# A replanned order of work, and layer 0's statistics partly by batch-norm instructions, in a two-layer residual block kernel

## Chip, core and metric

The kernel runs on one core of one Trainium2 chip. The metric is the time of one execution on the device, in microseconds (us). Five engines work side by side, each through its own queue of instructions in order: TensorE (PE; PEld is its weight load), VectorE (DVE), ScalarE (ACT), GpSimd (POOL) and SyncE (SP), which here issues nearly all transfers.

## What is computed

x has 128 batches of 128 rows by 512 columns in fp32; adj is 128 x 128. Layer 0 mixes rows, takes the row maximum and normalizes; layer 1 is masked attention with 8 heads over the 128 rows, a projection, an inner layer norm, and an outer one.

```
# layer 0: W1 = W2 = adj, so C - A is the bias and the same in every column
A   = adj @ x[b];  C = adj @ x[b] + b0
out = max over n of relu(A[n] + (C - A)[m])      # = relu(rowmax(A) + b0)
x   = layernorm(x + out)                          # out is one number per row
# layer 1
qkv = x @ w_qkv;  attn = softmax(mask(adj, q k^T / 8));  o = (attn v) @ w_proj + b_proj
x   = layernorm(x + o + layernorm(o) * gamma + beta)
```

## The kernel before

**Tiles and groups.** Batches go in 32 groups of four. For each batch: `conv` (L186) multiplies adj^T by x into one PSUM bank `pa`; `conv_max` (L190, DVE) takes the row maximum into `rm`; `relu_0` (L196, POOL) adds the bias. `add_0` (L202, ACT) adds rm to x in place and sums the row; `stats_0` (L484, ACT) makes the sum of squared deviations; `rstd_0` and `shift_0` (L213 to L225, L490, L491, POOL) make scale and shift for a pair of batches; `norm_0` (L232, ACT) applies them. `x_halves` (L244, ACT) writes x as two planes of 16-bit halves into the one buffer `xplanes`, SP stores them to DRAM (`rowsx`), and `crossbar_x` (L250, SP) brings them back transposed into an `xt` buffer. `split_x` (L261, L263 on DVE; `split_high`, L268 on POOL or L270 on ACT; `split_d`, L275 on POOL or DVE) makes the three forms of x (h, l, d) whose products stand for one fp32 product. In group 0 PE transposes x instead (`transpose_x`, L239), and `product_v` (L289) makes two of the values in plain fp32.

**Products.** `dense` (L309, L310, L317) makes for each group eight products of 512 columns for q and k (j = 4 to 11) and four for the values v (j = 0 to 3). Each has two PSUM banks, from the pool `ps_1` (four banks: names pm, pd) or `ps_2` (two buffers of two banks: name pp). `dense_main` (L344, ACT) and `dense_rest` (L348, DVE) empty them. `project` (o products) uses the same form, emptied by `projected_main` and `projected_rest` (DVE).

**Attention.** `scores` (L359, into `psc`), `masked` (L371, DVE: scale and add the mask), `row_max` (L379, DVE), `exps` (L386, ACT, eight of them), `weights` (L394, L395, DVE), `halves` (L401, ACT: planes of the weights, stored by SP as `rows`), `crossbar_T` (L410, SP: transposed back as `eT`), `attend` (L432, into `pav`), `heads` (a split of pav). In the last group PE transposes the weights (`transpose_e`, L419; `weights_T`, L423, ACT).

**End of layer 1.** `residual` reloads x (`xb`), `residual_x` (L455, L456, POOL) normalizes it again with the kept scale and shift and adds beta, `residual_o` (L473) adds o on POOL, in the last group on DVE. `stats` (squares on ACT, small operations on POOL), `norm_1` (L503, L478, DVE) and `norm_2` (L511, ACT, then the store by SP) finish.

**The order.** Nothing is left to a scheduler: every step is put into a list with a place in us by `at(place, f, ...)`, the list is sorted, and the steps are issued in that order on all engines' queues. PE's steps are laid end to end with the lengths in `LENGTH` (56.1 us a group in the plan), after `dense_order`, `pair_order` and `tail_order`. All other steps are placed relative to a PE step by the numbers in the table `O`, one per position in the group, and clamped so that nothing stands ahead of what it needs. `O["two"]` chooses engines and PSUM pools. A group's period in the plan runs from dense product (g, 4) to (g + 1, 4). In it PE does dense 4, 5, two convolutions, dense 6, 8, 7, 11, 10, 9, then attention, scores, dense 0 to 3 and four projections of two groups before, with the other two convolutions just ahead of the last.

**Buffers that couple queues.** `xt` has four buffers that x and its transposed form take in turn, so that the load of the next group's first x is placed right behind the group's fourth `crossbar_x`; `xplanes` and `planes` have one, `eT` two, `o` three (shared with the weights' raw tiles at the start).

Of the kernel before, what the change touches and what calls it, by code (L numbers as in the profile page):

```python
# [18 lines left out]
EPS = 1e-5  # L19
# [7 lines left out]
def tile_adj_resnorm_d2(  # L27
# [198 lines left out]

    def norm_0(b, vector=False):
        rstd, nm = norms.pop((b, 0))
        if vector:
            nc.vector.tensor_scalar(xs[b], xs[b], rstd, nm, op0=ALU.mult, op1=ALU.add)  # L230
            return
        nc.scalar.activation(xs[b], xs[b], AF.Identity, bias=nm, scale=rstd)  # L232
# [117 lines left out]
    def scores(b):  # L350
# [4 lines left out]
        pscs[b] = psc = ps_2.tile([P, 2, HP, P], FP, tag="ps2", name=f"psc_{b}")  # L355
        for hp in range(HP):
            for s in range(2):
# [3 lines left out]
                    start=True, stop=True,  # L361
                )

    def masked(b):
        if b < B - 1:
            e = work.tile([P, H, P], FP, tag="e", bufs=3, name=f"e_{b}")
        else:

            e = work.tile([P, 2, H * P], U16, tag="planes", bufs=1, name=f"e_{b}")
            e = e.rearrange("p s m -> p (s m)").bitcast(FP).rearrange("p (h m) -> p h m", h=H)  # L370
        nc.vector.scalar_tensor_tensor(  # L371
# [3 lines left out]
        es[b] = e  # L375

    def row_max(b):
        nmax = small.tile([P, H], FP, tag="nmax", name=f"nmax_{b}")
        nc.vector.tensor_reduce(nmax, es[b], AX.X, ALU.max, negate=True)  # L379
        es[b] = es[b], nmax  # L380

    def exps(b):
        e, nmax = es[b]
        sums = small.tile([P, H], FP, tag="sums", name=f"sums_{b}")
        for j in range(H):
            nc.scalar.activation(  # L386
                e[:, j, :], e[:, j, :], AF.Exp, bias=nmax[:, j : j + 1],
                accum_out=sums[:, j : j + 1],
# [82 lines left out]
    def residual_o(b):  # L471
        engine = nc.gpsimd if b < B - G else nc.vector
# [35 lines left out]
    def norm_2(b):  # L508
# [9 lines left out]
    O = {'add_0': [-28.01, -2.67, 12.08, -40.74],  # L518
 'conv_max': [4.55, 4.72, 6.29, 4.66],
 'dense_order': [('dense', 4), ('dense', 5), ('conv', 3), ('conv', 2), ('dense', 6), ('dense', 8),  # L520
                 ('dense', 7), ('dense', 11), ('dense', 10), ('dense', 9)],
 'final': {'norm_1': [5.56, 10.5, 14.34, 13.61],
           'norm_2': [12.82, 25.73, 75.6, 26.29],
           'residual': [-18.87, -9.5, -3.43, -8.74],
           'residual_o': [5.36, 6.15, 8.98, 4.31],
           'residual_x': [-41.8, -51.69, -15.49, -25.59],
           'stats_1': [5.17, 9.89, 7.71, 8.6],
           'stats_2': [12.28, 13.13, 19.78, 20.53]},
 'last': {'norm_1': [9.58, 9.14, 7.67, 8.6],
          'norm_2': [13.12, 22.67, 13.86, 10.82],  # L530
          'residual': [-2.72, -10.61, 6.62, -30.79],
          'residual_o': [3.24, 7.11, 7.11, 5.39],
          'residual_x': [-30.28, -1.34, -16.65, -32.32],
          'stats_1': [5.84, 4.73, 7.43, 4.32],
          'stats_2': [9.71, 14.36, 12.44, 9.12]},
 'load': [0.06, -0.01, -14.55, -3.61],
# [300 lines left out]
```

## Time and profile before

| | us |
|---|---|
| median of 3 runs | 1988.98 (1987.63 to 1991.59) |
| profiled execution, its own time | 1980.06 |
| its span | 1978.3 |
| dense product (3, 4) starts | 205.80 |
| dense product (31, 4) starts | 1869.74 |

| stretch, us | PE busy | DVE | ACT | POOL | granted clock |
|---|---|---|---|---|---|
| 0 to 205.8 | 174.65 | 157.83 | 156.07 | 97.92 | 0.98 |
| 205.8 to 1869.7 | 1605.23 | 1384.11 | 1410.46 | 1157.93 | 1.00 |
| 1869.7 to 1978.3 | 80.28 | 75.98 | 58.64 | 72.64 | 0.89 |

How its lines are read: in a wait, the engine and what it was to work on stand left of the arrow, what ended its idle time right of it; then us in total, how often, the longest. In a line of the timeline, start and length in us, engine (q for its queue), source line, operation, output and inputs, and in brackets the idle time before it with what ended it. In a line of groups, the count, then busy us in total and mean ns of one, then the idle time before them. An engine's output that the next engine takes up costs nothing as long as PE finds it in time.

### The profile page before, as it was taken

The page shows a single profiled execution, that of the slowest core. Times are in us where ns is not written, and L with a number is a line of the kernel's source. Part 1 is how long each engine was busy: PE and PEld are TensorE (multiplying, and loading weights), DVE is VectorE, ACT ScalarE, POOL GpSimd, SP SyncE. Part 2 cuts the span into 40 slices and gives each one's busy share as a digit, 9 for nine tenths or more (in the row PEclk, how much of TensorE's full clock was granted, in tenths as well). Part 3 has the DMA queues.
Part 4 walks back from the last instruction along what each step waited for, and adds up shares of the span by engine and source line. Part 5 has one row for each costly group of instructions (what it writes and reads, how often), then busy time and mean ns, then how long its engine had stood idle before and what let it go on. Part 6 is the DMA issues. An engine that isn't in the chain of part 4 may idle for free.

```text
span 1978.3 us, 33244 instructions
## 1 busy us (share of the span) xinstructions
PE 1860.2 (94%) x10537; PEld 1435.6 (73%) x10537; DVE 1617.9 (82%) x2485; ACT 1625.2 (82%) x4158; POOL 1328.5 (67%) x1970
## 2 busy tenths in 40 slices
PE   7799999999999999999999999999999999999995
PEld 4577777777777777777777777777777777777773
DVE  6788888878888888888878888877788878888885
ACT  5788888888888788888888888888888888878763
POOL 4166767766677766777766767766767766767767
PEclk9999999999999999999999999999999999999997
DMA  4465556665665665566675566665565675665541
GB/s 129 101 171 145 159 162 160 155 172 152 148 162 161 159 181 150 150 162 159 161 181 149 154 165 164 160 172 144 155 158 159 165 179 145 159 154 159 137 118 48
DMA packets 486144, 302.94 MB, mean 153 GB/s; under 512 B 399440, under 2 KB 403664, under 8 KB 485969
## 3 DMA queue, kind: packets, MB, share of 16 engines
q1 hardware_dynamic: 485104, 299.70, 58.5%
q8 instruction: 84, 1.38, 0.3%
q10 hardware_dynamic: 864, 1.12, 0.2%
q14 instruction: 92, 0.75, 0.1%
HBM read 72.16 MB, written 131.07 MB: 103 GB/s over the span
## 4 chain that ended last, share of the span: by engine, by line
PE 61%; ACT 14%; DVE 10%; DMA 8%; issue 5%; POOL 2%; SPq 0%; DVEq 0%; ACTq 0%; POOLq 0%
PE pa L186 5%; ACT e L386 4%; DMA xt<-in_x_dram 3%; DMA rowsx<-xplanes 2%; ACT xplanes L244 2%; ACT planes L401 2%; PE psc L359 2%; PE pav L432 2%; DMA eT<-rows 2%; ACT xt L232 2%; ACT square L484 1%; DVE x_l L263 1%; DVE xh L261 1%; DVE v L348 1%; DVE e L371 1%
## 5 line engine op out<-in xcount | busy, mean ns | idle before, releaser
L386 ACT ACTIVATE e<-e,nmax 128x128 f32<-128x128 f32 x1024 | 396.2, 391 | 74.1 <-DVE nmax L379 74.1
L490 POOL TENSOR_SCALAR sum<-sum 128x1 f32<-128x1 f32 (+1 forms) x322 | 102.1, 317 | 203.6 <-ACT square L484 188.4
L401 ACT COPY planes<-e 128x2048 uint16<-128x2048 uint16 x124 | 234.1, 1888 | 1.8 <-issue 1.8
L491 POOL TENSOR_TENSOR sum<-sum,mhalf 128x1 f32<-128x1 f32 (+1 forms) x322 | 212.8, 661 | 26.8
L484 ACT ACTIVATE square<-o,sum 128x512 bf16<-128x512 f32 x256 | 183.5, 717 | 24.1 <-DVE o L478 22.4
L386 ACT ACTIVATION_READ_ACCUMULATOR e<-e,nmax 128x1 f32 x1024 | 194.7, 190 | 0.0
L456 POOL TENSOR_TENSOR xb<-xb,beta_sb 128x512 f32<-128x512 f32 x128 | 176.9, 1382 | 10.7
L395 DVE TENSOR_TENSOR e<-e,sums 128x1024 f32<-128x1024 f32 x128 | 173.7, 1357 | 4.4
L432 PE MATMUL pav<-eT,v 128*64 128x128 f32 x2048 | 142.3, 282 | 32.8 <-DMA eT<-rows 18.1
L496 POOL TENSOR_SCALAR sum<-sum 128x1 f32<-128x1 f32 x256 | 100.5, 392 | 101.7 <-DVE o L478 99.1
L473 POOL TENSOR_TENSOR xb<-xb,o 128x512 f32<-128x512 f32 x124 | 161.9, 1306 | 4.8
L244 ACT COPY xplanes<-xt 128x1024 uint16<-128x1024 uint16 x124 | 129.3, 1043 | 31.6 <-DMA rowsx<-xplanes 29.6
L432 PEld LDWEIGHTS pav<-eT,v 128*64 128x64 f32 x2048 | 112.1, 138 | 59.4 <-DVE x_l L263 21.9
L379 DVE TENSOR_REDUCE nmax<-e 128x8 f32<-128x1024 f32 x128 | 154.9, 1211 | 0.0
L371 DVE SCALAR_TENSOR_TENSOR e<-psc,mask 128x1024 f32<-128x1024 f32 x128 | 152.9, 1214 | 0.7 <-PE psc L359 0.7
L186 PE MATMUL pa<-xt,adjT 128*128 128x512 f32 x256 | 123.9, 607 | 25.9 <-DMA xt<-in_x_dram 16.5
L455 POOL TENSOR_SCALAR xb<-xb,sum 128x512 f32<-128x512 f32 x128 | 127.2, 994 | 25.3 <-DMA xb<-in_x_dram 24.6
L359 PE MATMUL psc<-qkT 64*128 64x128 f32 x2048 | 142.0, 284 | 1.9 <-DVE e L371 1.9
L359 PEld LDWEIGHTS psc<-qkT 64*128 64x128 f32 x2048 | 123.4, 189 | 25.4 <-issue 23.0
L213 POOL TENSOR_SCALAR sum<-sum 128x2 f32<-128x2 f32 (+1 forms) x66 | 31.2, 472 | 161.9 <-ACT xt L202 161.6
L202 ACT ACTIVATE xt<-xt,rm 128x512 f32<-128x512 f32 x128 | 91.9, 718 | 43.8 <-POOL rm L196 43.8
L511 ACT ACTIVATE o<-o,sum 128x512 f32<-128x512 f32 x128 | 100.8, 814 | 23.9 <-POOL sum L499 23.8
(4653 smaller groups left out, 5770.0 us busy)
## 6 DMA issues: line engine op xcount, KB each, us to landing
rows<-planes SPq DMA_DIRECT2D x124, 512.0 KB, 3.3
xt<-in_x_dram SPq DMA_DIRECT2D x128, 256.0 KB, 3.5
xb<-in_x_dram SPq DMA_DIRECT2D x128, 256.0 KB, 2.9
out_dram<-o SPq DMA_DIRECT2D x128, 256.0 KB, 2.4
rowsx<-xplanes SPq DMA_DIRECT2D x124, 256.0 KB, 2.5
wraw<-in_L_gnn_w_qkv_dram SPq DMA_DIRECT2D x8, 256.0 KB, 3.2
xT<-rowsx SPq DMA_TRANSPOSE x124, 3.5
eT<-rows SPq DMA_TRANSPOSE x124, 4.8
```

The source lines that it names most:

```text
L186: nc.tensor.matmul(pa[b], adjT, xs[b], start=True, stop=True)
L244: nc.scalar.copy(planes, xs.pop(b).bitcast(U16).rearrange("p (m s) -> p s m", s=2))
L359: nc.tensor.matmul(psc[:, s, hp, :], qkT[hs, hp, i, :], qkT[hs, KC + hp, i, :], start=True, stop=True,)
L371: nc.vector.scalar_tensor_tensor(e, pscs.pop(b).rearrange("p s a m -> p (s a) m"), scale, mask_b, op0=ALU.mult, op1=ALU.add,)
L386: nc.scalar.activation(e[:, j, :], e[:, j, :], AF.Exp, bias=nmax[:, j : j + 1], accum_out=sums[:, j : j + 1],)
L395: nc.vector.tensor_tensor(e, e, sums[:, :, None].to_broadcast([P, H, P]), op=ALU.mult)
L401: nc.scalar.copy(planes, e.rearrange("p h m -> p (h m)").bitcast(U16).rearrange("p (m s) -> p s m", s=2),)
L432: nc.tensor.matmul(pavs[b][s * HD : (s + 1) * HD, hp, :], v[:, h * HD : (h + 1) * HD], eT[:, s * HP + hp, :], start=True, stop=True,)
L456: nc.gpsimd.tensor_tensor(xbs[b], xbs[b], beta_sb, op=ALU.add)
L473: engine.tensor_tensor(xbs[b], xbs[b], os[b], op=ALU.add)
L484: nc.scalar.activation(square, x, AF.Square, bias=s[:, 0:1], scale=-float(D), accum_out=s[:, 1:2],)
L491: nc.gpsimd.tensor_tensor(s, s, mhalf[:, :n], op=ALU.pow)
```

## The change

Four things, of which the first is by far the longest in effect on the order:

1. Nearly every number of `O` is new, so that the steps of all engines but PE change places. PE's order stays, apart from some exchanges in the tail. In `two`, dense product 0 of a group takes its banks from `ps_2`, the first projection takes two of `ps_1`; `split_d` of the second x goes from DVE to POOL, `split_high` of the first o from POOL to ACT; at the start two engines are swapped for a copy and a norm.
2. `stats_x`, `rstd_x`, `shift_x` are new: mean and variance of x by `bn_stats` and `bn_aggr` on DVE, without first adding rm (one number per row doesn't change what the normalization gives). The first pair of every group and all of group 0 use them; the second pairs keep `add_0` and `stats_0`.
3. `scores` can put the mask into PSUM by two products of the identity with the mask, ahead of the scores; `exps` then reads PSUM and scales. The last batch alone uses it.
4. In the last group `residual_o` of the first batch goes to POOL. Loads of x are placed after all four splits of the group are known, and the statistics after the loads.

```diff
+    def stats_x(b):
+        st = small.tile([P, 6], FP, tag="bnst", bufs=2, name=f"bnst_{b}")
+        nc.vector.bn_stats(st, xs[b])
+        nc.vector.bn_aggr(mv0s[g][:, i, 0:2], st)
+
+    def rstd_x(b, n):
+        var = mv0s[g][:, i : i + n, 1]
+        nc.gpsimd.tensor_scalar(var, var, EPS, None, op0=ALU.add)
+        nc.gpsimd.tensor_tensor(var, var, mhalf[:, :n], op=ALU.pow)
+
+    def shift_x(b, n):
+        mean, rstd, both, shift = (mv0s[g][:, i : i + n, k] for k in range(4))
+        r = rms[g][:, i : i + n]
+        nc.gpsimd.tensor_tensor(both, mean, r, op=ALU.add)
+        nc.gpsimd.tensor_tensor(both, r, both, op=ALU.subtract)
+        nc.gpsimd.tensor_tensor(shift, both, rstd, op=ALU.mult)
+        for k in range(n):
+            norms[b + k, 0] = c0s[b + k] = rstd[:, k : k + 1], shift[:, k : k + 1]
...
+        if with_mask:
+            for s in range(2):
+                nc.tensor.matmul(
+                    psc[:, s], ident, mask[:, None, :].to_broadcast([P, HP, P]), start=True, stop=False,
+                )
...
-    O = {'add_0': [-28.01, -2.67, 12.08, -40.74],
+    O = {'add_0': [-38.7, -4.55, -0.42, -31.04],
...
- 'load': [0.06, -0.01, -14.55, -3.61],
+ 'load': [-20.41, 3.65, -32.28, -8.94],
...
- 'softmax': {'cross': [-12.79, -9.61, -18.95, -6.28],
-             'exps': [10.86, 9.05, 42.17, 22.92],
-             'halves': [1.11, 11.24, 0.39, 2.34],
-             'masked': [0.34, 3.01, 1.47, 17.35],
-             'row_max': [16.52, 12.06, 18.4, 20.81],
-             'weights': [10.99, 14.73, 21.85, 34.94]},
+ 'softmax': {'cross': [-11.04, -10.0, -15.2, -5.92],
+             'exps': [13.59, 24.89, 35.29, 23.69],
+             'halves': [8.19, 11.44, 0.41, 1.44],
+             'masked': [2.1, 1.22, 6.73, 16.85],
+             'row_max': [28.59, 28.53, 20.89, 20.26],
+             'weights': [9.81, 15.04, 21.31, 31.4]},
...
- 'two': {'copy': [0, 1],
-         'd': [1, 0, 1, 0, 0, 1, 0, 1],
-         'dense': [0, 0, 0, 0, 1, 0, 1, 0, 0, 0, 0, 0],
+ 'two': {'bn': [1, 0],
+         'copy': [1, 0],
+         'd': [1, 1, 1, 0, 0, 1, 0, 1],
+         'dense': [1, 0, 0, 0, 1, 0, 1, 0, 0, 0, 0, 0],
...
-         'h': [1, 0, 0, 0, 1, 1, 0, 0],
-         'norm': [1, 0, 0, 0],
-         'po': [1, 0, 1, 0]},
- 'x_cross': [-8.02, -8.17, -10.06, 4.43],
+         'h': [1, 0, 0, 0, 0, 1, 0, 0],
+         'norm': [0, 1, 0, 0],
+         'po': [0, 0, 1, 0],
+         'tail_mask': [0, 0, 0, 1],
+         'tail_vector': [0, 1, 1, 1]},
+ 'x_cross': [-8.02, -4.16, -10.12, 2.24],
...
- 'x_halves': [-7.87, -8.53, -8.31, -7.49],
+ 'x_halves': [-8.29, -11.6, -7.53, -6.86],
...
+                    if two_of("bn", 0, i // 2):
+                        done = 0.0
+                        for k in pair:
+                            q = max(min(early[k][1], limit - 1.5), loads.get(k, pe["conv", k]) + 0.1)
+                            at(q, stats_x, k)
+                            done = max(done, q)
+                        at(done + 0.1, rstd_x, pair[0], 2)
+                        done = max(done + 0.2, r + 0.1, limit - 0.1 + min(O["rstd_0"][i], 0.0))
+                        at(done, shift_x, pair[0], 2)
...
+                            if k + G < B:
+                                loads[k + G] = max(splits[k] + max(O["load"][k % G], 0.02), crossed[b // G] + 0.02)
+                                at(loads[k + G], load_x, k + G)
...
-    for b, u in splits.items():
-        if b + G < B:
-            at(max(u + O["load"][b % G], u + 0.02, crossed[b // G] + 0.02), load_x, b + G)
```

## The prediction

> **What bounds the kernel now.** I read the page's summary and slices first, then what TensorE waits for in the steady part, then one group of four batches in order of time.
>
> ```profile
> PE 1860.2 (94%) x10537; PEld 1435.6 (73%) x10537; DVE 1617.9 (82%) x2485; ACT 1625.2 (82%) x4158; POOL 1328.5 (67%) x1970
> ...
> PE   7799999999999999999999999999999999999995
> ```
>
> TensorE (PE) is the bound, and it has holes at both ends. Groups start where dense product (g, 4) starts: (3, 4) at 205.80 and (31, 4) at 1869.74 us, so 28 groups last 59.43 us each. Busy time by stretch gives PE idle 31.2 us of the first 205.8, 58.7 us of the 1663.9 between, and 28.3 us of the last 108.6. PE's own waits from 200 to 1800 us:
>
> ```profile
> PE pav L432 <- DMA eT<-rows: 15.8, 17, 2.5
> PE pa L186 <- DMA xt<-in_x_dram: 15.8, 15, 1.8
> PE pav L432 <- DVE x_l L263: 6.7, 10, 0.8
> PE pa L186 <- DVE xh L261: 5.5, 6, 1.0
> PE pa L186 <- DVE x_l L263: 3.1, 2, 1.7
> PE pm_('o', 17)_3542 L309 <- ACT v L344: 1.0, 1, 1.0
> ```
>
> With the other nine rows like the last (v, 6.1 us in all) and three of 0.2 these are 54.6 us in 26.9 groups, 2.03 a group. Three places: attention times values (pav), the convolution (pa), the second projection. A group without them would take 57.4 us. The work of PE is the same after the change, apart from the tail, so only waits can go.
>
> Why are the transfers late? Group 10 starts at 622.52; times after "+" count from there. ScalarE (ACT), SP's queue and PE:
>
> ```profile
> 646.39 1.89 ACT L401 COPY planes<-e 128x2048 uint16<-128x2048 uint16 x1
> ...
> 653.76 1.05 ACT L244 COPY xplanes<-xt 128x1024 uint16<-128x1024 uint16 x1 [1.56 <-DMA rowsx<-xplanes]
> ...
> 659.70 1.03 ACT L244 COPY xplanes<-xt 128x1024 uint16<-128x1024 uint16 x1
> ...
> 668.25 1.05 ACT L244 COPY xplanes<-xt 128x1024 uint16<-128x1024 uint16 x1
> ```
>
> ```profile
> 660.76 0.34 SPq L246 DMA_DIRECT2D rowsx<-xplanes  x1
> 661.20 1.91 SPq L410 DMA_TRANSPOSE eT<-rows  x1
> ...
> 669.43 0.52 SPq L246 DMA_DIRECT2D rowsx<-xplanes  x1
> 673.55 1.23 SPq L250 DMA_TRANSPOSE xT<-rowsx  x1
> 674.83 1.04 SPq L91 DMA_DIRECT2D xt<-in_x_dram  x2
> ```
>
> ```profile
> 666.47 1.09 PE L432 MATMUL pav<-eT,v 128*64 128x128 f32 x16 [1.38 <-DMA eT<-rows]
> ...
> 678.31 1.96 PE L186 MATMUL pa<-xt,adjT 128*128 128x512 f32 x4 [1.05 <-DMA xt<-in_x_dram]
> ```
>
> SP's queue is in order. The last eT transpose is queued behind the store of the third xplanes, which ACT starts at +37.2; the next group's load of x is queued behind the store and transpose of the fourth, which ACT starts at +45.7. Both are ACT's lateness, passed through SP: its plan places are +32.8 and +41.9.
>
> **The change, part by part.**
>
> *Statistics.* Half of the batches (the first pair of each group, and all of group 0) lose two ACT passes:
>
> ```profile
> L202 ACT ACTIVATE xt<-xt,rm 128x512 f32<-128x512 f32 x128 | 91.9, 718 | 43.8 <-POOL rm L196 43.8
> ...
> L484 ACT ACTIVATE square<-xt,sum 128x512 bf16<-128x512 f32 x128 | 92.2, 721 | 1.0
> ...
> L190 DVE TENSOR_REDUCE rm<-pa 128x1 f32<-128x512 f32 x128 | 84.5, 680 | 3.1 <-PE pa L186 3.1
> ...
> L394 DVE RECIPROCAL sums<-sums 128x8 f32<-128x8 f32 x128 | 24.7, 193 | 0.3 <-ACT e L386 0.3
> ```
>
> Each pass is 0.72 plus 0.19 for the accumulator's read, so ACT loses 4 x 0.91 = 3.6 us a group, and 0.63 gets added for one "high" split moved to it from POOL (row of L270): -3.0. VectorE (DVE) gains two statistics instructions and two aggregations, which no trace here has run. Nearest rows: the 512-wide reduction (0.68) and the 8-wide reciprocal (0.19): 2 x 0.87 = 1.74 us; two passes over the data would make 3.1, and below 2 x 0.5 (the 0.46 of the leanest 512-wide row, L261, and no aggregation) it won't go. I take 1.74. One x_d subtraction of 1.16 (mean) leaves DVE, so DVE is +0.6 on some 50 us. POOL gets that x_d (1.30), loses the high split (1.98) and about 0.4 of small operations: -1.1. All this is behind PE; it counts only through the queues below.
>
> A rule bears on this: the Trainium skill, "SBUF — State Buffer", § Who interferes with whom, has a VectorE instruction with two SBUF inputs contend with a GpSimd one that reads SBUF, and the loser blocked for the whole instruction, while one with a single SBUF input outside the two-port modes does not contend. The trace fits the first half: x_d on DVE takes 0.68 at least and up to 1.72. The rule speaks against moving a further x_d to POOL: if it blocks one DVE instruction for all its length, DVE's +0.6 becomes +1.9; by the rows' means, which hold such blocking already, it stays +0.6. I take the rows; the statistics instruction, with one input, adds no blocking by the rule, which no row here shows.
>
> *ACT's order.* In the new order the halves of the previous softmax (1.8 us) go before +23.4 and not after it. From the same point, the last qkT eviction (645.90, +23.4), the new ACT queue up to the third xplanes is: eviction 0.5, norm 0.8, xplanes 1.0 (to +25.7), an add 0.8, a final norm 0.7, a square 0.8, the high split 0.6, norm 0.8 (to +29.3), xplanes 1.0 (its predecessor's store, issued +25.8, takes 2.5 to 3.6, so the 1.56 wait is gone), eight exps 3.1 from +30.3 (their row maximum was at +30.1), norm 0.7: the third xplanes starts at +34.1, 3.1 us earlier. Transpose issued at +35.7, landing after the 5.1 us that it took here (661.20 to 666.34): +40.8. PE, without its earlier waits, wants it at 665.09 - 0.52 = +42.05. The shortage of 1.4 becomes a slack of 1.2.
>
> On: eviction 0.5, exps from +36.6 (row maximum as before) to +39.7, eviction 0.5, square 0.8, norm 0.8: fourth xplanes at +41.8, 3.9 earlier. Softmax halves (1.8) now follow it, and their 512 KB store slips into SP ahead of the transpose; SP is then waiting for the xplanes store anyway. Store issued at +42.9 and landed at +47.0 (4.1 as before, 669.43 to 673.49), transpose 1.3, load at +48.3, landed +51.7 (3.35 as before); PE wants it at +52.84 (678.31 less the waits 1.05, 1.38, 0.52). Slack 1.1.
>
> Here a second rule gives another sum: "DMA: Bandwidth & Descriptors", § Anatomy of one DMA (stated for the GpSimd path), has a fixed 2.0 us plus bytes by 436 GB/s, 2.6 us for 256 KB. The page's list of issues has 3.5 for the load (nine in ten land by 3.8), 4.8 for eT (by 5.3). By the rule the load would have 1.9 us of slack and the later halves would be free; by the row 1.1, which a store in its way can use up now and then. I take the row.
>
> *New waits.* The second projection now waits for evictions of the first on DVE (planned 3 us before it) rather than for ACT's v: its 7.1 us go. The third projection now needs the buffer that the third mask-add frees, and that has moved behind other DVE work. From the row maximum's end (659.13, +36.6): weights 2.2, two evictions 0.6 each, split of x 1.1, v 0.6, projection 0.6, weights 1.5, heads 1.3, norm 1.5, split 0.9, split of x 1.1, mask-add 1.1: done at +49.7, wanted at +50.0. Level, so 0 to 1 us; I take 0.3.
>
> Sum per group: 2.03 off, 0.3 on, and 0.4 for landings beyond the slack: -1.3 us, for 28 groups -36. Bounds: -0.3 and -1.9.
>
> *Start.* The four layer-0 statistics leave ACT, but two of them stand on DVE ahead of adjT's copy, waiting for x 1 (landed 5.62): the first convolution moves from 4.83 to about 7.7. Against it, norms no longer wait for squares. Batch 0's norm follows its weight split on ACT, about 13.4; value product at about 17, as now (17.02). First dense product as now: 0. Then PE waits of 3.2, 1.4 and 3.0 for qkT evictions behind xplanes copies on ACT, which come earlier now: I take 5 of 7.6 off, bounds +3 and -12 with the other waits of groups 1 and 2.
>
> *Tail.* PE's largest wait (4.87 at 1936.80, for eT's copy behind a square that waited for DVE) loses that square; the 2.33 for POOL's high split moves to ACT. The mask of the last batch by PE adds two matrix products of the convolution's size, 2 x 0.86 = 1.7, and takes 1.2 off DVE. A final norm now stands ahead of that copy and can take some back. Of 7.2 I keep 6.7 - 1.7 = 5; bounds +4 and -14.
>
> Sum: 36 + 5 + 5 = 46. The profiled execution took 1980.06 us (span 1978.3), so 1934; the three runs' median is 8.9 above it, 1988.98 - 46 = **1943 us**.
>
> **Rivals.**
> - *Only half of it* (DVE becomes the limit). For: DVE is 83% busy in the middle stretch, would be 87%, and the mask-add has no slack. Against: it is idle about 10 us a group. At -0.5 a group, 14, and half of the ends, 5: 1970.
> - *It doesn't do what it says.* The load is still issued right behind the last transpose, with the same planned 2.1 us before its convolution; if ACT's order isn't what makes it late, the waits stay. For: the plan places; against: the 3 to 4 us of ACT above. Ends alone: 1984.
> - *Slower: the mask-add.* Ahead of it in DVE's queue stands the split of the second x, whose transpose the plan now issues 4 us later. If that stops DVE, everything behind (v, heads, evictions) is late, and PE at projection 3. Against: SP should issue it at about +38, for a use at +47.5. From 1.7 us of lateness per group (the 1.3 gained, 0.3 and the ends' 10/28) the change loses; at 3 us more, +47 net of the rest: 2026.
>
> **How the numbers follow.** Forecast 0.70, with its own range 1925 to 1957; half 0.17 (1957 to 1980); no effect 0.06 (1980 to 1993); slower 0.06; better than 1925 0.01. The range of 8 in 10, 1922 to 1973, leaves out the last two and part of the third. 0.2% (4 us) is about what a measurement tells from no change: faster (under 1985) 0.90, same 0.04, slower 0.06.
>
> **What would show it.** Groups of about 58.1 us; PE's waits for eT and xt under 10 us together from 200 to 1800; the third and fourth xplanes copies some 3 us earlier after dense (g, 4); statistics instructions near 0.7 us; the third projection waiting for DVE's e a few tenths; no 4.9 us wait for eT's copy in the tail. Wrong if projection 3 waits over 1.5 us a group, if the load still lands after its convolution's turn with ACT on time, or if DVE's queue is late throughout.

## The result, and the profile after

The changed kernel takes 1970.53 us (median of 4 runs, 1967.99 to 1971.78), the kernel before beside it 1990.28 (4 runs, 1987.63 to 1991.8): a ratio of 0.9901, 95% interval 0.9883 to 0.9918, 19.8 us less. 46 were forecast. On another chip the same pair gave 1968.49 and 1982.49, ratio 0.993 (0.9906 to 0.9954). Single runs of the kernel before lie between 1973 and 1995 us in one session, those of the changed kernel within 7 us; a pair of profiled executions therefore says less than the ratio. The profiled executions differ by 8.3 us of span only (1978.3 and 1970.0), since that of the kernel before was some 9 us faster than its median.

Summary and slices of the changed kernel's page, which answer to those of before:

```profile
PE 1868.6 (95%) x10541; PEld 1434.7 (73%) x10541; DVE 1647.6 (84%) x2585; ACT 1548.3 (79%) x3926; POOL 1244.1 (63%) x1935
...
PE   6799999999999999999999999999999999999995
```

ACT is busy for 76.9 us less and GpSimd for 84.4 less, DVE for 29.7 more. Dense product (3, 4) starts at 207.13 us (before 205.80), (31, 4) at 1864.83 (1869.74): 28 groups of 59.20 us each in place of 59.43. The start lost 1.3 us, the groups gained 6.2 and the tail 3.4.

TensorE's waits from 200 to 1800 us, changed kernel (us in total, times, longest):

```profile
PE pav L471 <- DMA eT<-rows: 9.7, 14, 1.7
PE pd_('o', 71)_11834 L344 <- POOL od L302: 1.6, 1, 1.6
PE pav L471 <- ACT xplanes L271: 1.4, 1, 1.4
PE pav L471 <- ACT xt L259: 1.3, 4, 0.4
PE pd_('o', 27)_4992 L344 <- POOL od L302: 1.0, 1, 1.0
PE pd_('o', 95)_15566 L344 <- POOL od L302: 1.0, 1, 1.0
```

The waits of the convolution for x and of the second projection for v are gone, that of the attention product is smaller. A new one stands in every group: the difference product of the fourth projection waits 1.0 us for od of GpSimd, 25.8 us in groups 3 to 28.

Group 10 after the change starts at 620.85 us. ScalarE:

```profile
646.33 0.81 ACT L259 ACTIVATE xt<-xt,sum 128x512 f32<-128x512 f32 x1 [1.43 <-POOL sum L250]
...
656.50 1.05 ACT L271 COPY xplanes<-xt 128x1024 uint16<-128x1024 uint16 x1
...
663.05 1.05 ACT L271 COPY xplanes<-xt 128x1024 uint16<-128x1024 uint16 x1
```

SP's queue, and TensorE in the same stretch:

```profile
658.01 2.05 SPq L449 DMA_TRANSPOSE eT<-rows  x1
...
667.92 2.07 SPq L91 DMA_DIRECT2D xt<-in_x_dram  x2
```

```profile
663.03 1.09 PE L471 MATMUL pav<-eT,v 128*64 128x128 f32 x16 [0.29 <-ACT xt L259]
673.72 1.88 PE L186 MATMUL pa<-xt,adjT 128*128 128x512 f32 x4
```

The third xplanes copy starts at +35.65 (before +37.2, forecast +34.1), the fourth at +42.2 (+45.7, forecast +41.8). The load of x is issued at +47.1 and has landed at +52.3, ahead of its convolution at +52.87, which has no wait. The last eT lands at +42.05, just too late. ScalarE's first norm of the group stands 1.43 us for GpSimd's shift, one of 27 such waits (39.4 us from 200 to 1800), and all that follows on ScalarE is late by it. GpSimd's queue shows why: the shift's last operation is the second line, behind one that waited 5.51 us for ScalarE.

```profile
643.35 0.19 POOL L529 TENSOR_SCALAR sum<-sum 128x1 f32<-128x1 f32 x1 [5.51 <-ACT square L523]
...
646.11 0.20 POOL L250 TENSOR_TENSOR sum<-sum 128x2 f32<-128x2 f32 x1
```

The end of the same group, GpSimd and then TensorE:

```profile
675.72 1.30 POOL L302 TENSOR_TENSOR x_d<-x_h,x_l 128x512 fp32r<-128x512 f32 x1 [0.70 <-ACT x_h L297]
676.98 1.44 POOL L302 TENSOR_TENSOR od<-oh,ol 128x512 fp32r<-128x512 f32 x1
```

```profile
678.48 1.19 PE L344 MATMUL pd_('o', 39)_6858<-p_d,od 128*128 128x512 f32 x4 [1.02 <-POOL od L302]
```

The difference of the third x now stands ahead of od in GpSimd's queue. In the plan od is at 4.84 us before the next group and x_d at 4.87; before the change od was first (-5.04 and -4.94).

### The profile page after: what moved, and what is told of

The parts are those of the page before. It is cut to its first block, busy times and chain, and to the rows that moved or that the text cites. A ratio compares the mean times of both kernels' runs of the same rounds, so it can differ in the third digit from the quotient of the medians.

```text
span 1970.0 us, 32988 instructions
## 1 busy us (share of the span) xinstructions
PE 1868.6 (95%) x10541; PEld 1434.7 (73%) x10541; DVE 1647.6 (84%) x2585; ACT 1548.3 (79%) x3926; POOL 1244.1 (63%) x1935
## 4 chain that ended last, share of the span: by engine, by line
PE 68%; POOL 11%; DVE 9%; issue 5%; ACT 4%; DMA 3%; SPq 0%; POOLq 0%; ACTq 0%; DVEq 0%
POOL x_d L302 5%; PE psc L391 4%; PE pav L471 4%; PE pa L186 3%; DMA eT<-rows 2%; POOL od L302 2%; DVE x_l L290 1%; DVE v L375 1%; POOL sum L530 1%; DVE xh L288 1%; ACT e L425 1%; DVE o L517 1%; ACT oh L297 1%; DVE o L542 1%; DVE o L503 1%
## 5 line engine op out<-in xcount | busy, mean ns | idle before, releaser
L529 POOL TENSOR_SCALAR sum<-sum 128x1 f32<-128x1 f32 (+1 forms) x287 | 58.3, 203 | 269.5 <-ACT square L523 256.4
L495 POOL TENSOR_TENSOR xb<-xb,beta_sb 128x512 f32<-128x512 f32 x128 | 210.7, 1646 | 10.7
L302 POOL TENSOR_TENSOR x_d<-x_h,x_l 128x512 fp32r<-128x512 f32 x97 | 125.7, 1311 | 140.2 <-DVE x_l L290 88.3
L530 POOL TENSOR_TENSOR sum<-sum,mhalf 128x1 f32<-128x1 f32 (+1 forms) x287 | 180.2, 628 | 23.8
L434 DVE TENSOR_TENSOR e<-e,sums 128x1024 f32<-128x1024 f32 x128 | 162.6, 1270 | 4.4
L542 DVE SCALAR_TENSOR_TENSOR o<-o,sum,gamma_sb 128x512 f32<-128x512 f32 x128 | 99.4, 777 | 76.4 <-POOL xb L512 72.9
L494 POOL TENSOR_SCALAR xb<-xb,sum 128x512 f32<-128x512 f32 x128 | 121.1, 946 | 35.0 <-DMA xb<-in_x_dram 33.1
L259 ACT ACTIVATE xt<-xt,sum 128x512 f32<-128x512 f32 x127 | 102.4, 806 | 46.3 <-POOL sum L250 45.4
```

The lines of the kernel that those rows point to most:

```text
L302: engine.tensor_tensor(fd, fh.bitcast(FP), fl.bitcast(FP), op=ALU.subtract)
L434: nc.vector.tensor_tensor(e, e, sums[:, :, None].to_broadcast([P, H, P]), op=ALU.mult)
L495: nc.gpsimd.tensor_tensor(xbs[b], xbs[b], beta_sb, op=ALU.add)
L530: nc.gpsimd.tensor_tensor(s, s, mhalf[:, :n], op=ALU.pow)
```

## The experiments

All are told by their ratio to the kernel before, run beside them. "Group" is the mean from dense (3, 4) to (31, 4) of the profiled execution.

### The parts of the change

**swap**: od goes ahead of the third x's difference on GpSimd, nothing else moves.

```diff
- 'o_d': [20.5, 7.73, 4.47, 10.06],
+ 'o_d': [20.5, 7.73, 4.47, 10.0],
```

> The changed kernel with one number of the plan moved by 0.06: on POOL the difference form of the fourth head output (od) goes ahead of that of the group's third x (x_d), as it stood before the change; nothing else moves. Theory A (the prediction's steady-state sum missed one wait: od queued behind x_d, which waits for ACT's x_h): od starts some 1.3 us earlier, the wait of 1.0 us at the fourth projection in every group goes, with its refill 1.3 us a group, 28 groups: the span falls from 1970.0 by 30 to 37 us, the median to about 1936. Rival B (TensorE takes back at another place what it gains here: x_d, now second, holds up dense product 4, or landings get short again as the period shrinks): 0 to 12 us. Rival C (the floor of a group has risen for another reason): no change within 4 us.

Measured 1960.65 us (1957.57 to 1961.98), ratio 0.9889 (0.9862 to 0.9915), group 58.85. The wait for od is gone, and another stands in its place at the next step: TensorE's first product of the next group waits for a bank that VectorE's second addition of the third projection frees, 0.85 us in most groups.

```profile
672.71 1.30 POOL L302 TENSOR_TENSOR od<-oh,ol 128x512 fp32r<-128x512 f32 x1 [0.16 <-ACT oh L297]
...
673.97 1.49 POOL L302 TENSOR_TENSOR x_d<-x_h,x_l 128x512 fp32r<-128x512 f32 x1
...
674.33 1.67 DVE L290 TENSOR_TENSOR x_l<-xT,xh 128x512 fp32r<-128x512 f32 x1
...
675.93 0.68 DVE L517 SCALAR_TENSOR_TENSOR o<-pp_('o', 38)_6795,o 128x512 f32<-128x512 f32 x1
...
676.76 0.47 PE L336 MATMUL pp_(11, 4)_6896<-x_h,w_h 128*128 128x512 f32 x1 [0.85 <-DVE o L517]
```

So two waits lay side by side, and the first hid the second. Of the 30 to 37 us of span expected by the first theory 10.4 came (1970.0 to 1959.6), which is rival B's size.

**order_alone**: the new order with the old statistics for the first pairs too (from group 1 on).

```diff
-  'two': {'bn': [1, 0],
+  'two': {'bn': [0, 0],
```

> The new plan, but the first pairs of groups 1 to 31 make their statistics by the two ACT passes again (group 0 keeps the batch-norm instructions). ACT has 3.6 us more a group, DVE 1.7 less. Theory A (ACT's lateness sets when the planes are stored, and so when transposed weights and x land): the four planes copies come 1.5 to 3.5 us later in the group, waits of TensorE for eT rise from 10 to 20 us or more in the steady part and waits for x return; the median is 10 to 40 us above that of the changed kernel. Rival B (the order alone gives the gain, ACT has room): within 5 us of the changed kernel. Rival D (the scale and shift behind the batch-norm instructions are what makes the first norm of a group late, by 1.4 us): faster than the changed kernel by 5 to 12 us.

Measured 2073.42 us, ratio 1.0459 (1.0427 to 1.049), group 62.64: 103 us above the changed kernel, where the first theory had 10 to 40. ScalarE's addition of rm now stands right ahead of eight exponentials and waits for GpSimd's relu; the exponentials, the weights and VectorE's evictions behind them are late, and TensorE waits at dense product 8:

```profile
ACT xt L202 <- POOL rm L196: 105.8, 26, 4.1
```

```profile
PE pd_(16, 8)_10086 L344 <- DVE qkT L375: 1.3, 1, 1.3
```

**order_late** asks whether that one place is to blame: the addition and squares are put right ahead of the norm.

```diff
-  'add_0': [-38.7, -4.55, -0.42, -31.04],
+  'add_0': [-0.5, -0.5, -0.42, -31.04],
...
-  'stats_0': [-4.77, 4.59, 27.53, -23.16],
+  'stats_0': [-3.0, -3.0, 27.53, -23.16],
```

> The new order with the old statistics of the first pair, once more, with ScalarE's addition and squares for them late, right before the norm, so that ScalarE does not stand 4.1 us behind GpSimd's relu as in the first of these. Theory (the order needs the instructions of the batch norm because they take 3.6 us off ScalarE where it is full): the 1.5 us of each group for the exponentials go, the norm comes 2 us later and the waits for eT grow: 2000 to 2040 us, slower than the kernel before. Rival (only the place was bad): 1985 us or less.

Measured 2039.19 us, ratio 1.0288 (1.0269 to 1.0308), group 61.29. The wait at product 8 is gone, product 9 waits 0.61 us for ScalarE and eT is late in nearly every group (25.8 us from 200 to 1800). One place made 34 us of the loss; with the better of the two places tried the order without the new statistics is still 58 us behind the kernel before.

**bn_alone** is the other half: the old numbers of O from group 1 on, with the batch-norm statistics of the first pairs, and the new start.

> The old plan from group 1 on and in the tail, with the batch-norm statistics for the first pair of each group, and the new plan for the start alone. Theory A (ACT's backlog): ACT is 3.6 us shorter a group, so the third and fourth planes copies come 1 to 3 us earlier and the waits for x and eT (31.6 us in the steady part before) fall to under 15; median 10 to 30 us below the kernel before. Rival B (the order does it, not the load of ACT): within 5 us of the kernel before. Rival D (DVE's added 1.7 us makes its queue late): slower by more than 5 us.

Measured 1985.2 us (20 runs), ratio 1.001 (0.9993 to 1.0026). The new instructions alone give nothing: the load of x and eT are as late as before (16.6 and 13.4 us). So this order needs the statistics, at least with the old ones in the two places tried, and the statistics pay through the order only.

**before_again** is the kernel before, for the scatter.

> The kernel before, unchanged, to see how its executions scatter: its profiled execution was 8.9 us below the median of its timed ones, that of the changed kernel was level with its own. If the order before leaves no slack for landings, its executions should scatter by several us with the landings, and a second profile should show waits for eT and xt that differ from the 31.6 us of the first by as much as the time differs; if profiling itself shortens it, this profile is about 9 us below the median again with the same waits.

Measured 1982.61 us (12 runs), ratio 0.9997 (0.9983 to 1.0011). Its profile has 25.5 us of waits for x and 10.7 for eT where the first had 15.8 of each: its waits are landings, and vary. The profiled execution took 1984.27 us, level with the median, so profiling itself does not shorten a run.

### What stands behind the first wait

**after_again** gives the changed kernel's time on another chip.

> The changed kernel once more, on the chip on which its variants are timed. Both theories: 1966 to 1976 us, 0.988 to 0.993 of the kernel before. TensorE waits about 1.0 us for od of GpSimd at the third product of every fourth projection, 26 us in groups 3 to 28.

Measured 1968.49 us (1966.96 to 1973.32), ratio 0.993; the wait for od 26.1 us in groups 3 to 28. As expected.

**rest** and **swaprest**: VectorE's second addition of the third projection goes ahead of the split of the fourth x, alone and together with the swap.

```diff
-  'po_rest': [-0.11, 1.17, 1.49, 0.32],
+  'po_rest': [-0.11, 1.17, 0.74, 0.32],
```

> The changed kernel with VectorE's second addition of the third projection ahead of the split of the fourth x, nothing else moved. Theory C (two waits lie in series at the end of a group: od, and behind it the bank that this addition frees; each hides the other): no gain alone, within 5 us of the changed kernel, because the 1.0 us for od stays. Rival D (the bank is not what TensorE lacks): the same time, and the third expectation below tells them apart.

> Both edits: od ahead of the x difference on GpSimd, and the second addition of the third projection ahead of the split of the fourth x on VectorE. Theory C: the 0.85 to 0.94 us at the start of a group goes, and the fourth projection with the step to the next takes about 3.2 us in place of 4.19, so 20 to 28 us below the swapped kernel's 1960.7, near 1935 us, ratio about 0.975. Rival D: the split of the fourth x, now 0.7 us later, is what the first product of the group waits for in its place, and the time stays within 8 us of the swapped kernel.

Measured: rest 1971.52 us, ratio 0.9937 (0.9915 to 0.9959), as expected; swaprest 1989.84 us, ratio 1.0039 (1.0025 to 1.0052), group 59.78: slower than before, where 1935 was expected. Both theories failed, the rival in its size (29 above the swap, not within 8). The 0.85 us is gone, but the fourth x's high part is 0.36 late for the first product, the two convolutions take 2.41 us in place of 1.36 to the start of dense product 6, which waits half a microsecond of it for VectorE's masked scores:

```profile
PE pp_(12, 6)_7583 L336 <- DVE sums L433: 0.9, 1, 0.9
PE pp_(6, 6)_3851 L336 <- DVE sums L433: 0.5, 1, 0.5
```

(The row names the reciprocal; what frees the bank is the mask-add ahead of it, which reads psc.)

**sr_stats**, **stats_only**, **swap_stats**: rsqrt and shift of the first pair go ahead of the layer norm statistics in GpSimd's queue, for which GpSimd idles 5.5 us; with both edits, alone, and with the swap.

```diff
-  'stats_0': [-4.77, 4.59, 27.53, -23.16],
+  'stats_0': [-4.77, -8.3, 27.53, -23.16],
```

> Both edits, and the rsqrt and shift of the first pair of x on GpSimd ahead of the layer norm statistics that they now stand behind, for which GpSimd idles 5.5 us. Theory: the shift is there 1.6 to 2.2 us earlier, the first norm on ScalarE no longer waits 1.4 us, the planes of all four x are copied earlier, and the 9 to 12 us that TensorE waits for eT and its cause shrink to under 5: 5 to 8 us below the kernel with both edits. Rival (eT is late for the transfers, not for ScalarE): within 2 us of it.

> The changed kernel with one edit: rsqrt and shift of the first pair of x on GpSimd ahead of the layer norm statistics of an earlier block; od is left behind the x difference. Theory E (the forecast's 0.4 us a group of residual landings is not a matter of transfers but of this place in GpSimd's queue): the 9 to 13 us of waits for eT and their cause go, and with them what scatters from group to group: 10 to 18 us below the changed kernel's 1968.5, near 1955 us, ratio 0.984 to 0.988; the groups are then all alike, near 58.5 us. Rival: eT is late for the crossbar transfer itself, and the time stays within 4 us of the changed kernel.

> This edit and od ahead of the x difference on GpSimd, VectorE's order as in the changed kernel. Theory E: the two gains add up, the swap's 8 to 10 us and 10 to 18 of the statistics: 1941 to 1952 us, ratio 0.977 to 0.984; groups near 58.2 us, the 0.85 us for VectorE's addition at the start of each group still there. Rival (VectorE sets the end of the group, whatever comes earlier): 1952 us or more.

Measured: sr_stats 1971.67 us, ratio 0.995 (0.9937 to 0.9964), 18 below swaprest, where 5 to 8 were expected; stats_only 1962.65, ratio 0.989 (0.9869 to 0.9912), 6 below the changed kernel's 1968.49 by the medians, group 58.81, less than expected; swap_stats 1945.25 (1943.34 to 1948.46), ratio 0.9808 (0.9786 to 0.983), group 58.33, as expected. In all three TensorE's waits for eT fall to 2 us or less from 200 to 1800, and groups are alike to 0.1 us but for a few. TensorE's waits in stats_only:

```profile
PE pav L471 <- ACT xplanes L271: 1.6, 2, 0.8
PE pd_('o', 71)_11834 L344 <- POOL od L302: 1.6, 1, 1.6
```

GpSimd's queue in stats_only, group 10: the rsqrt starts as soon as VectorE's statistics are there, and ScalarE's first norm starts without a wait.

```profile
641.96 0.23 POOL L240 TENSOR_SCALAR sum<-sum 128x2 f32<-128x2 f32 x1 [6.16 <-DVE sum L234]
...
643.50 0.20 POOL L250 TENSOR_TENSOR sum<-sum 128x2 f32<-128x2 f32 x1
```

The edited number belongs to VectorE's statistics in the plan, but these keep their place in VectorE's queue; what moves is GpSimd's rsqrt and shift. What looked like a late transfer was these five operations of two columns each, behind an instruction in GpSimd's queue that waited for ScalarE.

### VectorE's stretch at the end of a group

**ss_main**: swap_stats, with VectorE's first addition of the third projection behind the split of the fourth x.

```diff
-  'po_main': [0.29, -1.52, 0.85, -1.05],
+  'po_main': [0.29, -1.52, 1.85, -1.05],
```

> The last, with VectorE's first addition of the third projection behind the split of the fourth x, in place of ahead of it, as in the kernel before; both additions then follow the split. Theory F (at the end of a group VectorE works without a break, and two of its operations take 1 us longer where GpSimd subtracts at the same time): the split starts 0.6 us earlier and has less of GpSimd's subtraction beside it, so that the 0.85 us at the start of the group shrinks to 0.2 to 0.5: 10 to 18 us below the last kernel. Rival (the sum of VectorE's work stays, so the second addition ends when it did): within 4 us of it.

Measured 1978.12 us, ratio 0.9977 (0.9966 to 0.9988), 33 above swap_stats where 10 to 18 less were expected. The wait at the start of the group is 1.57 us. GpSimd and VectorE at the end of group 11:

```profile
736.15 1.30 POOL L302 TENSOR_TENSOR od<-oh,ol 128x512 fp32r<-128x512 f32 x1 [0.17 <-ACT oh L297]
737.40 1.49 POOL L302 TENSOR_TENSOR x_d<-x_h,x_l 128x512 fp32r<-128x512 f32 x1
```

```profile
735.14 0.42 DVE L288 TENSOR_SCALAR xh<-xT 128x512 int32<-128x512 int32 x1
735.60 0.69 DVE L290 TENSOR_TENSOR x_l<-xT,xh 128x512 fp32r<-128x512 f32 x1
736.21 1.52 DVE L288 TENSOR_SCALAR xh<-xT 128x512 int32<-128x512 int32 x1
737.77 1.67 DVE L290 TENSOR_TENSOR x_l<-xT,xh 128x512 fp32r<-128x512 f32 x1
739.37 0.68 DVE L503 SCALAR_TENSOR_TENSOR o<-pp_('o', 42)_7417,bias_sb 128x512 f32<-128x512 f32 x1
```

The same two instructions take 0.42 and 0.69 us on the third x, and 1.52 and 1.67 on the fourth, where each ends 0.3 to 0.6 us after GpSimd's subtraction beside it. The additions, which read PSUM and one SBUF operand, are not held: the 61 of the changed kernel that start while GpSimd works on two 512-wide operands (200 to 1800 us) take 0.67 to 0.69 us. The edit moved the first addition from beside the subtraction and put the split there.

**ss_main_row**: that, and the row maximum of the third scores (1.2 us of VectorE) moved to ahead of the fourth projection's source, where VectorE idles 1.0 us.

```diff
-             'row_max': [28.59, 28.53, 20.89, 20.26],
+             'row_max': [28.59, 28.53, 10.0, 20.26],
```

> The last, with the row maximum of the third block's scores (1.2 us of VectorE) taken from behind the x difference to ahead of the split of the fourth projection's source, where VectorE idles 1.0 us. Theory F: VectorE's unbroken stretch at the end of a group is 1.2 us shorter and starts 0.2 later, the exponentials of the next softmax start earlier; TensorE's own wait at the start of the group is not shortened by it, so 0 to 6 us below the last kernel. Rival (the row maximum delays the projection's source by more than the idle time covers): 0 to 10 us above it.

Measured 1980.21 us, ratio 0.9989 (0.9976 to 1.0001), 2 above ss_main and not below it. The wait at the start of the group grows to 1.77 us, by the 0.2 us that the row maximum is longer than the idle time, and the convolutions take 1.31 us in place of 1.75. The mean group is 59.42 us in both kernels. Work taken from behind the addition does not bring it earlier.

**d_only** and **stats_d**: the third x's difference is formed by VectorE, behind its second addition, so that GpSimd has od alone; the second has the early shift too.

```diff
-         'd': [1, 1, 1, 0, 0, 1, 0, 1],
+         'd': [1, 1, 0, 0, 0, 1, 0, 1],
...
-  'x_d': [7.79, -15.76, -5.19, -19.02],
+  'x_d': [7.79, -15.76, 1.9, -19.02],
```

> The changed kernel with one edit: the difference of the third x is formed by VectorE (behind the second addition of the third projection) in place of GpSimd, so that od is alone on GpSimd there. Theory G (what TensorE loses at the end of a group is GpSimd's two subtractions in a row: od stands behind one, and VectorE's split of the fourth x, which reads and writes SBUF alone, is held while they run, xh 0.93 to 1.5 us for 0.42, x_l 1.67 for 0.69): od is in time, the split takes its 1.1 us but for what od covers, and the second addition comes a microsecond earlier, so that both the 1.0 us for od and the 0.85 us behind it go: 28 to 38 us below the changed kernel's 1968.5, 1930 to 1941 us, ratio 0.974 to 0.979. Rival (VectorE is full at the end of a group, and 0.7 us more of it is paid by TensorE): 1958 us or more.

> The same, and rsqrt and shift of the first pair of x ahead of the layer norm statistics on GpSimd. Theory G: groups of 57.4 us in place of 58.2, none of the waits of the end of a group left: 1917 to 1928 us, ratio 0.966 to 0.973. Rival: the 0.85 us for VectorE's addition stays or comes back at the next step as in the two kernels that moved the additions: 1940 us or more.

Measured: d_only 1978.21 us, ratio 0.9985 (0.9972 to 0.9998); stats_d 1959.87, ratio 0.989 (0.9869 to 0.991). Both 30 us and more above what theory G said. The wait at the start of the group is 0.36 us in place of 0.85, the convolutions take 2.21 to the start of product 6, which waits 0.34 of it for the masked scores: what was won at one step is lost at the next.

**stats_d_row** and **ss_row**: the row maximum moved as above, in stats_d and in swap_stats.

> The kernel with both edits (third x difference on VectorE, rsqrt and shift of the first pair early on GpSimd), and the row maximum of the third block's scores (1.2 us of VectorE) taken from behind the differences to ahead of the fourth projection's source, where VectorE idles 1.0 us. Theory H (from the source of the fourth projection to the masked scores of the next group VectorE works 13 us without a break, 0.9 us longer than TensorE between the same two points, so each shuffle inside that stretch only moves the wait, and only work taken out of it pays): the pair of graph convolutions takes 1.3 us again in place of 2.2, the 0.34 us behind it go, the wait at the start of the group grows by 0.2: groups near 57.6 us, 18 to 26 us below that kernel's 1959.9, 1934 to 1942 us, ratio 0.976 to 0.981. Rival (the row maximum ahead of the split costs at the start of the group what it saves behind): within 6 us of 1960.

> The kernel of 1945.2 us (od ahead of the x difference on GpSimd, rsqrt and shift of the first pair early) with the row maximum moved in the same way. Theory H: its wait at the start of the group (0.85 us) ends with VectorE's second addition, which stands ahead of the row maximum's old place and is not helped; it grows by the 0.2 us that the row maximum is longer than the idle time: 0 to 8 us above 1945.2. Rival (the stretch as a whole sets the group): 10 us or more below it.

Measured: stats_d_row 1941.75 us (1939.25 to 1943.18), ratio 0.9748 (0.9724 to 0.9772), group 58.11; ss_row 1950.63, ratio 0.9797 (0.9776 to 0.9818). By the ratio 28 us came off stats_d (18 by the medians, on another chip, and 17 by the group), and ss_row equals swap_stats within the noise. Both times lie where theory H had them. What TensorE still waits for in stats_d_row:

```profile
PE pav L471 <- DMA eT<-rows: 1.8, 2, 1.6
PE pp_(20, 4)_12494 L336 <- DVE o L517: 1.4, 1, 1.4
PE pp_(30, 4)_18714 L336 <- DVE o L517: 0.5, 1, 0.5
```

The stretch can be measured: from VectorE's ol of the fourth projection, which TensorE releases by finishing the third, to TensorE's dense product 6. Inside it TensorE needs two things of VectorE: the bank that the second addition of the third projection frees, for dense product 4, and the mask-add, which frees the bank of product 6. Medians over groups 4 to 28, us; the ends are counted from the start of ol:

| kernel | second addition ends | mask-add ends | stretch | set by | median group |
|---|---|---|---|---|---|
| before | 4.74 | 12.92 | 13.31 | waits for x | 59.26 |
| after | 6.59 | 13.44 | 13.73 | addition, od | 58.89 |
| rest | 3.67 | 13.39 | 13.54 | mask-add | 58.81 |
| swap | 6.10 | 12.95 | 13.24 | addition | 58.43 |
| swaprest | 3.67 | 14.12 | 14.27 | mask-add | 59.51 |
| stats_only | 6.58 | 13.40 | 13.72 | addition, od | 58.69 |
| sr_stats | 3.67 | 14.12 | 14.27 | mask-add | 59.12 |
| swap_stats | 6.10 | 12.92 | 13.23 | addition | 58.21 |
| ss_main | 6.82 | 14.25 | 14.40 | mask-add | 59.28 |
| ss_main_row | 6.82 | 13.12 | 13.96 | addition | 59.15 |
| d_only | 5.58 | 13.47 | 13.62 | mask-add | 58.89 |
| stats_d | 5.57 | 13.47 | 13.62 | mask-add | 58.50 |
| stats_d_row | 5.57 | 12.34 | 12.71 | addition | 57.87 |
| ss_row | 6.10 | 12.80 | 13.24 | addition | 58.40 |

"Addition" stands where product 4 starts 0.15 us after the addition has ended and product 6 follows 6.99 us later, TensorE's own time for products 4 and 5 and the convolutions. "Mask-add" stands where product 6 starts 0.15 us after the mask-add has ended. One of the two holds in every kernel but before. The group is the stretch and 44.9 to 45.3 us more, again but for before (46.0) and for order_alone and order_late (48.6 and 47.2), which wait elsewhere too.

This is what the shuffles did. The swap ended the addition 0.49 us earlier (the fourth x's high part takes 0.92 us in place of 1.45 beside GpSimd), and the stretch is shorter by just that. Putting the addition ahead of the split ended it at 3.67, and the mask-add became the later one. The row maximum stands between the two: moved out, it shortens the stretch by 0.91 us in stats_d and by 0.44 in ss_main, where the mask-add came last, and by nothing in swap_stats, where the addition did. (In its new place it makes ol 0.2 us later, and products 6 and 8 take back another 0.1 in the first two, so that the median groups change by -0.63, -0.13 and +0.19.) So neither the order nor the amount of work in the stretch counts as such, only what stands ahead of the instruction that TensorE waits for. Nor does a full queue show it: VectorE is busy in all of the stretch but 0.2 to 0.4 us in every row, before included (13.06 of 13.31 us), where TensorE waited for x.

## Why the prediction was wrong in its size

**What bounds it, and ACT's order: right.** The chain from ScalarE's third and fourth planes through SP to eT and x was the cause of the waits: moved 1.6 and 3.5 us forward, it took the waits for x away altogether (slack forecast 1.1 us, 52.87 - 52.3 = 0.6 in group 10). The third xplanes copy moved by half of what was forecast, as GpSimd's shift is missing from the queue that was added up.

**Statistics: right for the new instructions, off in what ACT loses and in one choice.** The two instructions had no row:

```profile
L233 DVE BATCH_NORM_STATS2 bnst<-xt 128x6 f32<-128x512 f32 x66 | 45.3, 687 | 1.2 <-DMA xt<-in_x_dram 1.2
...
L234 DVE BATCH_NORM_AGGREGATE sum<-bnst 128x2 f32<-128x6 f32 x66 | 12.0, 182 | 2.3
```

0.687 and 0.182 us: 1.74 a group, as taken. An ACT pass and its accumulator's read overlap in the trace: the next instruction starts 0.71 us after the pass, not 0.91. So four passes are 2.8 us and not 3.6, and with the high split (0.52 in this way) ACT's busy time fell by 2.3 us a group (1410.46 to 1346.46 over 28), not 3.0. GpSimd's fell by 2.8, not 1.1. VectorE's grew by 1.0 us a group in the middle stretch (1384.11 to 1412.58 over 28), not 0.6. The forecast weighed the Trainium skill's "SBUF — State Buffer", § Who interferes with whom, and took the rows' means. The rule was the better guide to the place: what counts is not the mean but which instruction stands beside which. In the kernel before the split of the fourth x started first (group 10, 678.63 us) and took 0.42 and 0.69 us; od, started at 679.11, took 1.82 us for its usual 1.30. In after the split starts while GpSimd subtracts, and takes 1.45 and 1.64. Before, VectorE, GpSimd and VectorE's second addition, then after:

```profile
678.63 0.42 DVE L261 TENSOR_SCALAR xh<-xT 128x512 int32<-128x512 int32 x1
679.08 0.69 DVE L263 TENSOR_TENSOR x_l<-xT,xh 128x512 fp32r<-128x512 f32 x1
...
679.11 1.82 POOL L275 TENSOR_TENSOR od<-oh,ol 128x512 fp32r<-128x512 f32 x1
...
680.41 0.69 DVE L478 SCALAR_TENSOR_TENSOR o<-pp_('o', 38)_6785,o 128x512 f32<-128x512 f32 x1
```

```profile
675.85 1.45 DVE L288 TENSOR_SCALAR xh<-xT 128x512 int32<-128x512 int32 x1
677.34 1.64 DVE L290 TENSOR_TENSOR x_l<-xT,xh 128x512 fp32r<-128x512 f32 x1
678.90 0.68 DVE L517 SCALAR_TENSOR_TENSOR o<-pp_('o', 38)_6795,o 128x512 f32<-128x512 f32 x1
```

From 200 to 1800 us in after, the 27 x_l that start while GpSimd works on two 512-wide operands have a median of 1.64 us, the other 82 of 0.69; the row maximum, with one input, has 1.21 in both cases (79 and 29), as the rule has it. The same section names one-input operations in a two-port mode as contenders, and that whoever comes first holds the other; xh, at 0.42 us the leanest of 512 columns, is held. Of the statistics instruction no case beside such an operation was seen.

**New waits: the step that failed.** "Sum per group: 2.03 off, 0.3 on, and 0.4 for landings beyond the slack" puts the fourth projection at nothing. By TensorE's steps, means over groups 3 to 28, before to after: attention product 2.98 to 2.59, third projection with the convolution behind it 5.21 to 4.30, dense product 1 from 3.10 to 2.80, that is 1.60 off of the 2.03, close to the forecast's 2.03 less 0.4. On it, fourth projection 3.24 to 4.55, 1.31 on, which the sum does not have; the third projection's 0.3 came to 0.04. With 0.06 of small changes the sum is -0.2 where -1.3 was forecast. (Profiles taken again, before_again and after_again, have 59.51 and 59.18 us a group, -0.3.)

Two things make the 1.31. GpSimd's queue was read for what leaves it and what comes to it ("POOL gets that x_d (1.30), loses the high split"), not for the order of od and x_d, which are 0.03 us apart in the plan: this is the 1.0 us for od. And VectorE's queue was followed to the third mask-add and not to the second addition of the third projection, which ends 4.74 us after ol in before and 6.59 in after, because GpSimd's subtractions hold the split ahead of it. Either of the two alone starts the next group late. In the swap od was in time, the addition late, and of 1.31 only 0.36 came back; in rest the addition was early and od late, and product 4 still started 6.53 us after ol in place of 6.74.

The 57.4 us of "a group without them" were not far off. In before, the waits for x lie in the stretch measured above, and the four of its 25 groups without a wait over 0.2 us there have a stretch of 12.72 to 13.11 us (before_again: four, 12.72 to 13.07). With the 45 us that the other kernels take for the rest, an estimate from these figures is 57.7 to 58.1 us for a group of the old order without waits. The new order has 13.73 in place of 12.7 to 13.1. The rival "half of it (DVE becomes the limit)" gave 1970, and that the number came out is luck: VectorE was one of two causes, but the reason given for it was an average of busy time, and GpSimd was not in it.

What was to show the forecast came in the main (no wait for x, 9.7 us for eT, xplanes earlier, 0.7 us for the statistics, the tail's longest wait shorter), and none of its signs of being wrong did: none of them looked at the fourth projection.

**Residual landings: right number, wrong cause.** 0.4 a group was put down to transfers that land late now and then. It measured 0.47, and moving two steps of GpSimd's queue took it to 0.07 and less. GpSimd's queue ahead of the first norm was in none of the steps.

**Start**: 5 us less were forecast, 1.3 more came. The forecast counted qkT evictions; what came up in the trace is dense product (1, 6), which waits 6.3 us for masked scores where it waited 2.3. This was not tested. **Tail**: 5 forecast, 3.4 came; the largest wait is eT's copy still, 3.0 us in place of 4.87.

**Slips in the rivals' sums.** "Ends alone: 1984" takes half of the ends' 10 us off; all of it makes 1979. The three terms of the slower rival's threshold add up to 2.0 us, not 1.7, and 3 us a group is 38 us net of the 46, not 47. VectorE's 87% is 86% with its own +0.6. None of it moves the forecast.

## What to carry to other kernels

When an edit takes away a wait of TensorE's, look at once for the next release behind it: for each product, how long its operands and its bank have been ready when it starts. The instruction that ended just before the product (0.15 us here) is the one that sets the pace, and only work ahead of it in its queue pays; an engine that is busy without a break need not be the limit. Read an in-order queue position by position for steps planned within a tenth of a microsecond of each other, the engine with the most idle time included. Put operations that read PSUM, not those between SBUF operands, beside GpSimd's subtractions, where the trace shows the latter held.

## What the runs showed that was not expected

Five operations of 0.2 to 0.7 us each matter even in the queue of GpSimd, which is idle for 37% of the time: moved ahead of one that waits 5.5 us, they were worth 6 us on the changed kernel and 15 to 18 where another wait had been removed (1960.65 to 1945.25, 1989.84 to 1971.67), so gains of edits do not add up in either direction. And stats_d_row, which is the changed kernel with three numbers and one engine of the plan altered, is at 0.9748 of the kernel before, where the change itself is at 0.9901 and 0.993.
